# Mamba layer on one core: B products in two row groups of TensorE, C products in four column groups, units of half the channels

## The chip, the cores and the metric

The kernel runs on one core of a Trainium2 chip. The metric is the device time of one execution in microseconds (us). Before the change it is 13144.94 us, the median of three runs (13144.44 to 13147.74). A core has five engines that run side by side, each with its own queue of instructions in order: TensorE (PE; the loads of its stationary operand are shown as PEld), VectorE (DVE), ScalarE (ACT), GpSimd (POOL) and SyncE (SP), which here only issues DMA transfers. TensorE writes into PSUM, eight banks of 512 floats in each of 128 partitions; everything else lies in SBUF or in HBM.

## The reference

The input x has the shape (16, 64, 64, 128). Layer 0 adds to x a two-dimensional recurrent network over the group-normed x; layer 1 adds the sum of a forward and a backward Mamba scan over the group-normed result, with 4096 tokens an image. The change lies in layer 1 alone. Cut to what matters:

```python
def _mamba(x, in_w, conv_w, conv_b, x_w, dt_w, dt_b, A_log, D, out_w):
    xz = x @ in_w.T
    xc, z = jnp.split(xz, 2, axis=-1)
    ...
    xc = jax.nn.silu(jnp.transpose(xt, (0, 2, 1)))
    dbl = xc @ x_w.T
    dt, Bm, Cm = jnp.split(dbl, [DT_RANK, DT_RANK + D_STATE], axis=-1)
    dt = jax.nn.softplus(dt @ dt_w.T + dt_b)
    dA = jnp.exp(dt[..., None] * A)
    dBx = dt[..., None] * Bm[:, :, None, :] * xc[..., None]
    def step(h, inp):
        dA_t, dBx_t, C_t = inp
        h = dA_t * h + dBx_t
        y = jnp.einsum('bds,bs->bd', h, C_t)
        return (h, y)
    ...
    y = jnp.swapaxes(ys, 0, 1) + xc * D
    y = y * jax.nn.silu(z)
    return y @ out_w.T
```

For each of 16 states and 256 channels there is thus: a decay (exp), a drive (dt times x times B), a recurrence along the tokens, a product with C, and a sum over the states.

## The kernel before, in words

Layer 0 runs first. Layer 1 works in 256 passes: 16 images, 2 directions, 8 chunks of 512 tokens. In a pass the 256 channels are two halves of 128 partitions, and tokens lie along the free axis, but for the sums, which stand with tokens on partitions.

What one pass does, with the names of its methods: `conv` (line 1049) and `silu` (1060) make xc; `xproj` (1087) makes dt's input, B and C as rows, in two column groups of 64, each for one half of the tokens; `rows` (1103) writes B and C to HBM; `dtproj` (1137) and `softplus` (1148) make dt; `times` (1154, GpSimd) makes dtx = dt * xc; `turn` and `turn_take` (1161, 1170) make its transpose dtxt.

For each state s and half h, `decay` (1180, ACT) writes exp(dt * A) into SBUF (`das`) or a PSUM bank (`da`). The drive is made in one of three ways, by a letter for each state in `KINDS`: "P", GpSimd multiplies dtx with a row of B that a DMA spread over all partitions (`drive`, 1185); "M" and "T", ACT scales dtxt by B, token by token (`drive_turned`, 1192, with B's transpose from `bturn`, 1112), and TensorE transposes it back (`drive_back`, 1218); "N" and "U", B's row is scattered to a diagonal in HBM and loaded as `dg`, and TensorE multiplies dtxt with it (`drive_back`, 1209). `scan` (1230, VectorE) runs the recurrence over 512 tokens; its start value comes from `carry`, which `keep` (1245 or 1249) writes after the same scan of the pass before. `out_of` multiplies with a spread row of C, on GpSimd for both halves at once (1256) or, for "T" and "U", on VectorE (1258). `sums` (1265) adds the 16 products of a pass in PSUM (`py`) by transposes with the identity: 8 for each state. `skip`, `again`, `finish`, `back`, `project` and the rest complete the output.

The order of the instructions is made by a planner in the kernel (`order_of_issue` and `simulate`): it knows a cost of each step (`COST`), a due time (`URGENCY`), the number of buffers (`RINGS`) and how many PSUM banks each use may hold (`LIMIT`), and lists the steps in the order in which its own model would start them. Six PSUM banks serve all short uses, and two hold `py`. Queues keep that order on the chip and wait for one another by semaphores.

Of the kernel before, what the change touches and what calls it, by code (L numbers as in the profile page):

```python
# [14 lines left out]
P = 128  # L15
# [5 lines left out]
NH = DI // P  # L21
# [15 lines left out]
KINDS = ("MPNTMNPMUNPTMNPM", "MPMTPNMPTMPUMNPM")  # L37

RINGS = {
    "bank": 6, "py": 1, "das": 4, "dbx": 4, "dbt": 3, "dg": 3, "hst": 4, "hc": 5,  # L40
    "br": 4, "cr": 5, "xc": 2, "dt": 2, "dtx": 2, "dtxt": 2, "dbl": 2, "bt": 2, "z": 1, "y": 1,
    "yt": 1, "xr": 1, "xl": 1, "yo": 1, "yl": 1,
# [3 lines left out]
    "conv": 0.865, "gate": 0.87, "silu": 0.62, "softplus": 0.65, "gate_take": 0.6, "dtproj": 0.95,  # L46
    "xproj": 1.0, "xproj_take": 0.4, "bturn": 0.25, "bturn_take": 0.15, "times": 2.34,
    "turn": 0.47, "turn_take": 0.47, "decay": 0.62, "drive": 2.34, "drive_turned": 1.6,
    "drive_back": 0.44, "drive_back_diag": 0.88, "scan": 1.18,
    "keep_turned": 0.13, "keep": 0.6, "out_turned": 0.6, "out": 2.34, "sums": 0.88, "skip": 0.44,  # L50
# [7 lines left out]
LIMIT = {"misc": 2, "bank": 5}  # L58
# [6 lines left out]
        {(0, 0): -27.9, (0, 1): -55.24, (0, 2): -37.14, (0, 3): -26.5, (1, 0): -25.66, (1, 1): -31.09,  # L65
         (1, 2): -28.23, (1, 3): -24.41},
        {(0, 0): -34.48, (0, 1): -62.91, (0, 2): -27.86, (0, 3): -25.86, (1, 0): -33.52, (1, 1): -26.55,
         (1, 2): -34.72, (1, 3): -27.13},
    ),
    "xproj": (  # L70
        {(): -7.14},
        {(): 5},
    ),
    "xproj_take": (
        {(): -0.87},
        {(): -6.61},
    ),
    "rows": (
        {(): 6.65},
        {(): 22.72},  # L80
    ),
    "bturn": (
        {(): -69.81},
        {(): -79.06},
    ),
    "bturn_take": (
        {(): -11.43},
        {(): -18.91},
    ),
    "dtproj": (  # L90
        {(0,): -63.21, (1,): -27.76},
        {(0,): -42.3, (1,): -15.88},
    ),
    "times": (
        {(): -134.9},
        {(): -152.1},
    ),
    "turn": (
        {(0,): -117.7, (1,): -95.41},
        {(0,): -92.29, (1,): -73.14},  # L100
    ),
    "turn_take": (
        {(0,): -12.62, (1,): -21.64},
        {(0,): -15.32, (1,): -17.24},
    ),
    "decay": (
        {(0, 0): 1.62, (0, 1): -12.81, (1, 0): -13.82, (1, 1): -8.37, (2, 0): 9.59, (2, 1): 7.54,
         (3, 0): -3.93, (3, 1): -3.12, (4, 0): -25.4, (4, 1): 2.96, (5, 0): 16.41, (5, 1): 14.98,
         (6, 0): -14.89, (6, 1): -7.22, (7, 0): 17.61, (7, 1): 6.71, (8, 0): -49.21, (8, 1): -31.38,
         (9, 0): 30.2, (9, 1): 28.66, (10, 0): -15.29, (10, 1): -11.14, (11, 0): -39.1, (11, 1): -52.04,  # L110
         (12, 0): 11.3, (12, 1): 12.04, (13, 0): -4.72, (13, 1): -9.28, (14, 0): -8.46, (14, 1): 9.15,
         (15, 0): 6.51, (15, 1): 10.38},
        {(0, 0): -11.72, (0, 1): -13.95, (1, 0): -23.83, (1, 1): -23.36, (2, 0): 5.39, (2, 1): 3.65,
         (3, 0): -27.89, (3, 1): -33.87, (4, 0): -17.63, (4, 1): -10.29, (5, 0): -5.06, (5, 1): 8.98,
         (6, 0): -5.94, (6, 1): 4.1, (7, 0): 5.44, (7, 1): 12.02, (8, 0): -73.78, (8, 1): -77.71,
         (9, 0): 21.8, (9, 1): 10.89, (10, 0): -3.99, (10, 1): -15.28, (11, 0): -27.37, (11, 1): -37.65,
         (12, 0): 21.39, (12, 1): 9.09, (13, 0): -2.78, (13, 1): -3.97, (14, 0): -1.99, (14, 1): 19.81,
         (15, 0): 11.27, (15, 1): 19.92},
    ),
    "spread": (  # L120
        {("c", 0): -1.78, ("c", 1): -117.27, ("b", 1): -23.09, ("c", 2): -80.12, ("d", 2): -40.37,
         ("c", 3): -18.07, ("c", 4): -0.55, ("c", 5): -99.41, ("d", 5): -52.16, ("c", 6): -133.17,
         ("b", 6): -13.49, ("c", 7): -18.83, ("c", 8): -39.5, ("d", 8): 9.08, ("c", 9): -42.09,
         ("d", 9): -26.61, ("c", 10): -81.5, ("b", 10): -14.43, ("c", 11): -35.04, ("c", 12): -76.62,
         ("c", 13): -69.54, ("d", 13): 21.06, ("c", 14): -21.91, ("b", 14): -26.12, ("c", 15): -95.57},
        {("c", 0): -14.51, ("c", 1): -135.28, ("b", 1): -22.37, ("c", 2): -75.2, ("c", 3): 26.76,
         ("c", 4): -11.36, ("b", 4): -10.82, ("c", 5): -37.95, ("d", 5): 9.47, ("c", 6): -122.31,
         ("c", 7): -91.31, ("b", 7): -6.34, ("c", 8): -1.04, ("c", 9): -15.62, ("c", 10): -118.12,
         ("b", 10): -20.57, ("c", 11): -6.63, ("d", 11): 42.13, ("c", 12): -104.85, ("c", 13): -62.16,
         ("d", 13): 36.52, ("c", 14): -56.98, ("b", 14): -28.81, ("c", 15): -80.03},  # L130
    ),
    "drive_turned": (
        {(0,): 4.39, (3,): 8.43, (4,): -6.7, (7,): -0.75, (11,): 7.02, (12,): -6.99, (15,): -17.26},
        {(0,): -1.81, (2,): -23.9, (3,): -35.33, (6,): -11.17, (8,): -20.91, (9,): -60.49, (12,): 7.71,
         (15,): 0.83},
    ),
    "drive_back": (
        {(0, 0): 3.71, (0, 1): 1.89, (2, 0): -5.19, (2, 1): -6.19, (3, 0): -4.81, (3, 1): 0.01,
         (4, 0): -2.71, (4, 1): 0.38, (5, 0): -18.47, (5, 1): 5.45, (7, 0): 9.18, (7, 1): 10, (8, 0): 9.85,
         (8, 1): 10.09, (9, 0): 10.62, (9, 1): 10.75, (11, 0): 3.53, (11, 1): 12.69, (12, 0): 4.21,  # L140
         (12, 1): 14.29, (13, 0): 12.99, (13, 1): 14.53, (15, 0): 16.89, (15, 1): 17.89},
        {(0, 0): -2.14, (0, 1): -4.49, (2, 0): -12.32, (2, 1): 4.91, (3, 0): -12.93, (3, 1): -0.55,
         (5, 0): -12.51, (5, 1): -4.37, (6, 0): -3.25, (6, 1): -2.4, (8, 0): 4.69, (8, 1): -1.16,
         (9, 0): 7.45, (9, 1): 9.75, (11, 0): 10.55, (11, 1): 10.75, (12, 0): 11.8, (12, 1): 14.97,
         (13, 0): 16.19, (13, 1): 16.9, (15, 0): 18.18, (15, 1): 10.8},
    ),
    "scan": (
        {(0, 0): 70.25, (0, 1): 59.47, (1, 0): 8.22, (1, 1): 9.32, (2, 0): -9.21, (2, 1): -2.84,
         (3, 0): 51.28, (3, 1): 75.32, (4, 0): 55.73, (4, 1): 59.47, (5, 0): 137.02, (5, 1): 138.28,
         (6, 0): 27.09, (6, 1): 15.69, (7, 0): 32.24, (7, 1): 37.07, (8, 0): 94.24, (8, 1): 108.17,  # L150
         (9, 0): 0.44, (9, 1): 28.19, (10, 0): 73.98, (10, 1): 59.24, (11, 0): 106.87, (11, 1): 94.54,
         (12, 0): -14.38, (12, 1): 5.54, (13, 0): 148.93, (13, 1): 161.13, (14, 0): 96.47, (14, 1): 100.3,
         (15, 0): 3.43, (15, 1): -30.56},
        {(0, 0): 96, (0, 1): 81.85, (1, 0): 21.08, (1, 1): 15.17, (2, 0): -6.35, (2, 1): 2.5,
         (3, 0): 36.94, (3, 1): 50.72, (4, 0): 106.56, (4, 1): 99.08, (5, 0): 93.31, (5, 1): 110.65,
         (6, 0): -9.88, (6, 1): -0.78, (7, 0): 31.56, (7, 1): 34.1, (8, 0): 112.12, (8, 1): 144.28,
         (9, 0): -41.6, (9, 1): -10.42, (10, 0): 40.85, (10, 1): 31.68, (11, 0): 26.81, (11, 1): 19.41,
         (12, 0): 6.38, (12, 1): 39.24, (13, 0): 149.38, (13, 1): 149.05, (14, 0): 81.27, (14, 1): 88.98,
         (15, 0): 50.57, (15, 1): 7.33},
    ),  # L160
    "keep": (
        {(0,): -45.32, (1,): -38.3, (2,): -27.42, (3,): 18.46, (4,): -29.29, (5,): -21.12, (6,): -34.06,
         (7,): -33.8, (8,): -42.14, (9,): -10.39, (10,): -80.29, (11,): 59.69, (12,): -29.07,
         (13,): -54.07, (14,): -50.65, (15,): 7.31},
        {(0,): -50.47, (1,): -36.77, (2,): -54.91, (3,): 44.96, (4,): -38.14, (5,): -61.49, (6,): -11.86,
         (7,): -26.15, (8,): 8.91, (9,): 9.26, (10,): -17.81, (11,): -47.77, (12,): -17.89, (13,): -57.38,
         (14,): -65.8, (15,): 6.8},
    ),
    "out_of": (
        {(0,): 42.48, (1,): -101.16, (2,): -79.47, (3, 0): -31.43, (3, 1): -28.02, (4,): 51.12,  # L170
         (5,): 18.82, (6,): -90.94, (7,): -54.6, (8, 0): 19.29, (8, 1): 24.04, (9,): -47.79, (10,): -28.65,
         (11, 0): -12.07, (11, 1): -5.85, (12,): -67.16, (13,): -35.58, (14,): 28.33, (15,): -59.17},
        {(0,): 31.38, (1,): -101.73, (2,): -8.51, (3, 0): -36.58, (3, 1): -37.73, (4,): 25.8, (5,): -6.07,
         (6,): -58.81, (7,): -73.64, (8, 0): -9.83, (8, 1): 5.81, (9,): -32.35, (10,): -90.84,
         (11, 0): 16.76, (11, 1): 25.57, (12,): -65.96, (13,): -59.82, (14,): -25.53, (15,): -3.11},
    ),
    "sums": (
# [1224 lines left out]
```

## Time and profile before

| what | value |
|---|---|
| median of three runs | 13144.94 us |
| span of the profiled execution | 13233.8 us |
| PE busy, share of the span | 12901.2 us, 97% |
| DVE busy | 12067.0 us, 91% |
| ACT busy | 11513.4 us, 87% |
| POOL busy | 11261.4 us, 85% |
| DMA moved | 2025.28 MB |
| mean granted TensorE clock | 0.993 |

Shares of the whole span mix the two layers: layer 0 lasts to about 1590 us and leaves ACT and POOL half idle. Matmuls are pipelined, so the mean duration of one is longer than the distance to the next, and a busy PE is not PE at its peak. A group's line names the line of the kernel, the engine, the operation, out<-in with buffer numbers left out, the shapes, the count, then busy us and mean ns, then the idle time of the engine just before these instructions and what ended it.

### The profile page before, as it was taken

The numbers are of one execution on the slowest core, as the hardware profiler recorded it, in microseconds if no ns is written. First come the engines' busy times: TensorE is split into PE (matmuls) and PEld (weight loads), VectorE is DVE, ScalarE is ACT, GpSimd is POOL, SyncE is SP. The second block draws the span as 40 slices with busy tenths as digits, with TensorE's granted clock in tenths as the row PEclk, the third lists the DMA queues.
The fourth block names the chain that finished last, engine by engine and source line by source line (L and its number), as shares of the span: only waits on it lengthen the run. The fifth ranks groups of instructions, "written<-read, shape, count | busy, mean of one in ns | idle before, by whom it ended". The sixth has DMA issues, their size and how long they took to land. (4 is left out here: it accounts for less than half of the span.)

```text
span 13233.8 us, 263820 instructions
## 1 busy us (share of the span) xinstructions
PE 12901.2 (97%) x91444; PEld 10833.0 (82%) x91444; DVE 12067.0 (91%) x14353; ACT 11513.4 (87%) x21184; POOL 11261.4 (85%) x4996
## 2 busy tenths in 40 slices
PE   8999999999999999999999999999999999999999
PEld 7666788888888888888888888888888888888887
DVE  6776699999999999999999999999999999999998
ACT  3444599999999999999999999999999999999998
POOL 0111299999999999999999999999999999999998
PEclk8999999999999999999999999999999999999999
DMA  4222265656666666656566666666665656666665
GB/s 143 54 57 54 63 172 158 172 156 172 161 167 165 164 165 160 172 158 172 158 170 161 166 165 163 166 159 172 158 173 160 169 162 168 164 163 166 163 166 145
DMA packets 2777751, 2025.28 MB, mean 153 GB/s; under 512 B 1584848, under 2 KB 1930464, under 8 KB 2776416
## 3 DMA queue, kind: packets, MB, share of 16 engines
q1 hardware_dynamic: 2698464, 1973.16, 57.5%
q10 hardware_dynamic: 77952, 35.24, 1.1%
q8 instruction: 725, 11.88, 0.4%
q14 instruction: 610, 5.00, 0.1%
HBM read 1849.24 MB, written 157.02 MB: 152 GB/s over the span
## 5 line engine op out<-in xcount | busy, mean ns | idle before, releaser
L1256 POOL TENSOR_TENSOR hc<-hst,cr 128x1024 f32<-128x1024 f32 x3328 | 7800.2, 2374 | 327.7 <-DVE hst L1230 243.2
L1230 DVE TENSOR_TENSOR_SCAN hst<-das,carry,hps 128x512 f32<-128x512 f32 x3808 | 4668.3, 1261 | 190.3 <-PE hps L1218 93.8
L1265 PE MATMUL py<-ident,hc 128*128 128x128 f32 x32768 | 4150.1, 274 | 57.2 <-POOL hc L1256 56.5
L1265 PEld LDWEIGHTS py<-ident,hc 128*128 128x128 f32 x32768 | 3676.6, 141 | 451.7 <-issue 272.5
L1180 ACT ACTIVATE das<-dt,A_log_sb 128x512 f32<-128x512 f32 x5888 | 3875.9, 713 | 121.5 <-DVE hst L1230 79.2
L1192 ACT ACTIVATE dbt<-dtxt,bt 128x256 f32<-128x256 f32 x7680 | 3231.7, 498 | 159.0 <-PE hps L1218 146.9
L1185 POOL TENSOR_TENSOR dbx<-dtx,br 128x1024 f32<-128x1024 f32 x1152 | 2724.6, 2378 | 10.1
L1230 DVE TENSOR_TENSOR_SCAN hst<-da,carry,dbx 128x512 f32<-128x512 f32 x2016 | 2468.8, 1260 | 31.7 <-ACT da L1180 30.0
L1218 PE MATMUL hps<-ident,dbt 128*128 128x128 f32 x15360 | 2264.2, 274 | 133.8 <-DVE hc L1258 109.3
L1209 PE MATMUL hps<-dg,dtxt 128*128 128x128 f32 x16384 | 2175.2, 277 | 38.7 <-DVE hst L1230 20.2
L1218 PEld LDWEIGHTS hps<-ident,dbt 128*128 128x128 f32 x15360 | 1783.9, 141 | 463.6 <-issue 329.7
L1209 PEld LDWEIGHTS hps<-dg,dtxt 128*128 128x128 f32 x16384 | 2004.6, 192 | 119.1 <-DVE hst L1230 45.9
L1049 PE MATMUL pp<-xT,wk 128*128 128x512 f32 x4096 | 1900.9, 596 | 0.5 <-DVE xl L837 0.5
L1230 DVE TENSOR_TENSOR_SCAN hps<-das,carry,hps 128x512 f32<-128x512 f32 x1344 | 1654.3, 1265 | 20.3 <-PE hps L1209 10.6
L1180 ACT ACTIVATE da<-dt,A_log_sb 128x512 f32<-128x512 f32 x2304 | 1556.2, 683 | 79.7 <-DVE hst L1230 58.6
L816 POOL TENSOR_TENSOR a_f<-a_f,c 128x288 f32<-128x288 f32 (+40 forms) x254 | 211.6, 833 | 1341.2 <-ACT a_f L808 1274.0
L1258 DVE TENSOR_TENSOR hc<-hps,cr 128x512 f32<-128x512 f32 x1536 | 1025.2, 674 | 258.5 <-DMA cr<-rows 247.7
L1049 PEld LDWEIGHTS pp<-xT,wk 128*128 128x128 f32 x4096 | 716.5, 190 | 627.7 <-issue 605.3
L1154 POOL TENSOR_TENSOR dtx<-dt,xc 128x1024 f32<-128x1024 f32 x256 | 607.9, 2374 | 280.4 <-ACT dt L1148 275.5
L1230 DVE TENSOR_TENSOR_SCAN hst<-das,hps 128x512 f32<-128x512 f32 x544 | 641.6, 1203 | 82.8 <-issue 27.1
L808 ACT ACTIVATE a_f<-pg_f,b_sb 128x288 f32<-128x288 f32 (+40 forms) x508 | 217.3, 471 | 361.9 <-DMA x<-xl 161.5
L1137 PE MATMUL pv<-dbl,dt_wT 128*128 128x256 f32 x2048 | 507.2, 380 | 8.5 <-ACT xc L1060 8.5
(115 smaller groups left out, 12672.9 us busy)
## 6 DMA issues: line engine op xcount, KB each, us to landing
cr<-rows SPq DMA_DIRECT2D x4096, 256.0 KB
br<-rows SPq DMA_DIRECT2D x1152, 256.0 KB
dg<-diag SPq DMA_DIRECT2D x1024, 256.0 KB
yf<-yo SPq DMA_DIRECT2D x128, 512.0 KB
yl<-yf SPq DMA_DIRECT2D x128, 512.0 KB
carry<-hst SPq DMA_DIRECT2D x3328, 1.0 KB
xs<-in_x_dram SPq DMA_DIRECT2D x64, 512.0 KB
xr<-x SPq DMA_DIRECT2D x128, 256.0 KB
```

The lines of the kernel that those rows point to most:

```text
L1049: nc.tensor.matmul(self.ps["conv", h], lhsT=wk[:, k, h * P : (h + 1) * P], rhs=xT[self.b % 2][:, t0 : t0 + T], start=(k == 0), stop=(k == ...
L1137: nc.tensor.matmul(pv[:, q * TQ : (q + 1) * TQ], lhsT=dt_wT[:, q, h * P : (h + 1) * P], rhs=self.dbl, start=True, stop=True,)
L1154: nc.gpsimd.tensor_mul(self.dtx, self.dt, self.xc)
L1180: nc.scalar.activation(t, self.dt[:, h, :], AF.Exp, scale=amat[:, h, s : s + 1])
L1185: nc.gpsimd.tensor_mul(t, self.dtx, bc(self.brow.pop(s), 1, NH))
L1192: nc.scalar.activation(t[:, j, :], self.dtxt[:, j, :], AF.Copy, scale=self.bt[:, j, s : s + 1])
L1209: nc.tensor.matmul(t[:, j * P : (j + 1) * P], lhsT=self.dtxt[:, j, h * P : (h + 1) * P], rhs=self.dbt[s][:, j, :], start=True, stop=True,)
L1218: nc.tensor.transpose(t[:, j * P : (j + 1) * P], self.dbt[s][:, j, h * P : (h + 1) * P], ident)
L1230: nc.vector.tensor_tensor_scan(t[:, self.rev], self.da.pop((s, h))[:, self.rev], dbx[:, self.rev], 0.0 if self.first else carry[:, self.d, ...
L1256: nc.gpsimd.tensor_mul(self.hc[s], self.hst[s], bc(self.crow[s], 1, NH))
L1258: nc.vector.tensor_mul(self.hc[s][:, h, :], self.h[s, h], self.crow[s])
L1265: nc.tensor.matmul(self.py[:, j, cols], start=j not in self.banks, stop=last, skip_group_check=True, **how,)
```

## The change

The three ways by letters go. Of the 16 states the first eight (`NX`) form two groups of four ("X"), the other eight four pairs ("R"), and every unit works on one half of the channels. `ORDER` lists the units' scans.

- X: GpSimd makes the drives of two states at a time into a tile `group` of 512 tokens by 4 states, state innermost, so each write steps over 16 bytes. The decay goes to a PSUM bank; the scan runs in place in `group`. TensorE transposes `group` in blocks of 32 tokens by 4 states (`turned`), ACT copies the block out of PSUM (`turned_take`), and `weigh` multiplies it with a matrix that holds C's four rows on shifted diagonals (`cd`), which is the product with C and the sum over the four states in one. Each of its matmuls has 32 stationary columns and writes 32 partitions; four stand side by side in four column groups.
- R: one matrix `dg` holds two states' B for 64 partitions above and 64 below; `drive_rows` multiplies dtxt with it in two row groups of 64 partitions, each writing its own PSUM bank of a two-bank tile `pair`. dtxt is made with a step of four tokens, `dg`'s columns are read with a step of four floats, and the two states lie alternating in `pair`. The decays go to SBUF. `out_of` multiplies two states with two spread rows of C on GpSimd, `sums` is as before.
- `dtproj` uses two row groups and the `pair` tile; `silu` and `softplus` are two sessions on ACT, between which decays may stand. `keep` is a DMA for each unit. `bturn`, `drive_turned`, VectorE's `out_of` and `keep` go.
- Rings: four banks in place of six, one `pair` of two banks; `y` and `yo`, `xl` and `xr` share buffers. Due times are new throughout.

```diff
-KINDS = ("MPNTMNPMUNPTMNPM", "MPMTPNMPTMPUMNPM")
+GX = 4
+TB = P // GX
+NX = 8
+NG, NR = NX // GX, (NS - NX) // 2
+ORDER = ("00a00b11c11d22e22f33g33h", "00a00b11c11d22e22f33g33h")
 RINGS = {
-    "bank": 6, "py": 1, "das": 4, "dbx": 4, "dbt": 3, "dg": 3, "hst": 4, "hc": 5,
-    "br": 4, "cr": 5, "xc": 2, "dt": 2, "dtx": 2, "dtxt": 2, "dbl": 2, "bt": 2, "z": 1, "y": 1,
-    "yt": 1, "xr": 1, "xl": 1, "yo": 1, "yl": 1,
+    "bank": 4, "pair": 1, "py": 1, "das": 3, "dg": 3, "group": 3, "cd": 2, "ht": 6, "hst": 3, "hc": 4,
+    "br": 3, "cr": 2, "xc": 2, "dt": 2, "dtx": 2, "dtxt": 2, "dbl": 2, "z": 1, "y": 1,
+    "yt": 1, "xl": 1, "yl": 1,
 }
...
-LIMIT = {"misc": 2, "bank": 5}
+LIMIT = {"misc": 2, "bank": 2}
...
+            def dtproj(self):
+                pv = self.ps["dt"] = psum.tile([P, NQ, T], F32, name=f"pv_{self.nm}", tag="pair")
+                for h in range(NH):
+                    for q in range(NQ):
+                        rows = slice(q * QP, (q + 1) * QP)
+                        nc.tensor.matmul(
+                            pv[:, q, h * TQ : (h + 1) * TQ],
+                            lhsT=dt_wT[rows, h * P : (h + 1) * P],
+                            rhs=self.dbl[rows, :],
...
+                strided = self.dtx.rearrange("p h (i j) -> p h j i", j=NB)
                 for j in range(2):
                     for h in range(NH):
                         nc.tensor.transpose(
-                            pt[:, j, h * P : (h + 1) * P],
-                            self.dtx[:, h, (2 * i + j) * P : (2 * i + j + 1) * P],
-                            ident,
+                            pt[:, j, h * P : (h + 1) * P], strided[:, h, 2 * i + j, :], ident
                         )
...
+            def drive(self, q, h):
+                g, m = divmod(2 * q, GX)
+                if m == 0:
+                    self.group[g, h] = ring(sp, "group", [P, T, GX], f"group_{self.nm}_{g}_{h}")
+                both = self.group[g, h].rearrange("p t m -> p m t")
+                nc.gpsimd.tensor_mul(both[:, m : m + 2, :], bc(self.dtx[:, h, :], 1, 2), self.brow[q])
+                for k in range(2):
+                    self.dbx[2 * q + k, h] = both[:, m + k, :]
...
+            def drive_rows(self, g, h):
+                step = P // NQ
+                dg = self.mat["d", g].rearrange("p (i n j) -> p j i n", n=2, j=NB)
+                pair = psum.tile([P, NQ, T], F32, name=f"hps_{self.nm}_{g}_{h}", tag="pair")
                 for j in range(NB):
+                    for r in range(NQ):
+                        rows = slice(r * step, (r + 1) * step)
+                        half = pair[:, r, :].rearrange("p (i j n) -> p j i n", j=NB, n=2)
                         nc.tensor.matmul(
+                            half[:, j, :, :],
+                            lhsT=self.dtxt[rows, j, h * P : (h + 1) * P],
+                            rhs=dg[rows, j, :, :],
                             start=True,
                             stop=True,
+                            skip_group_check=True,
                         )
+                for k in range(2):
+                    self.dbx[NX + 2 * g + k, h] = pair.rearrange("p r t -> p (r t)")[:, k::2]
...
+            def out_of(self, g, h):
+                self.hc[g, h] = ring(sp, "hc", [P, 2, T], f"hc_{self.nm}_{g}_{h}")
+                nc.gpsimd.tensor_mul(self.hc[g, h], self.hst[g, h], self.crow[g])
+
+            def turned(self, g, h, j, place):
+                pt = self.ps["turned", g, h, j] = bank(place, f"ptg_{self.nm}_{g}_{h}_{j}", (P, GX, P))
+                for k in range(GX):
+                    t0 = (GX * j + k) * TB
+                    nc.tensor.transpose(
+                        pt[:, k, :],
+                        self.group[g, h][:, t0 : t0 + TB, :].rearrange("p t s -> p (t s)"),
+                        ident,
+                    )
+
+            def turned_take(self, g, h, j):
+                t = self.ht[g, h, j] = ring(sp, "ht", [P, GX, P], f"ht_{self.nm}_{g}_{h}_{j}")
+                nc.scalar.copy(t, self.ps.pop(("turned", g, h, j)))
+
+            def weigh(self, g, h):
+                cd = self.mat["k", g].rearrange("p (k t) -> p k t", t=TB)
+                for j in range(NB):
+                    for q in range(GX):
+                        c0 = (j % 2) * DI + h * P
                         nc.tensor.matmul(
+                            self.py[q * TB : (q + 1) * TB, j // 2, c0 : c0 + P],
+                            lhsT=cd[:, GX * j + q, :],
+                            rhs=self.ht[g, h, j][:, q, :],
+                            start=False,
+                            stop=False,
+                            skip_group_check=True,
                         )
```

## The prediction

> **What bounds the kernel now.** I read the busy time by stretches first, then the scan's first and last start, the groups, the order of time on TensorE around the tiled matmuls, and at last VectorE's groups by shape, for operands that step over 16 bytes.
>
> Layer 1 runs from the first scan to the last. Line 1230 by itself (duration shortest/median/longest in ns, first and last start):
>
> ```profile
> L1230 DVE TENSOR_TENSOR_SCAN hst<-das,carry,hps x3808: 1242/1256/1282, 1636.1 to 13217.6; 128x512 f32<-128x512 f32 x191
> ...
> L1230 DVE TENSOR_TENSOR_SCAN hst<-das,hps x544: 1187/1196/1222, 1595.4 to 12888.0; 128x512 f32<-128x512 f32 x182
> ```
>
> So (13217.6 - 1595.4) / 256 = 45.40 us for one pass; the 1595 us before belong to layer 0, which the change leaves alone. A stretch in the middle of layer 1 (busy time of PE, weight loads, DVE, ACT, POOL, clock, DMA):
>
> ```profile
> 6000.00:8000.00 2000.00, 1958.45 (x14555) 1677.64 (x14554) 1896.51 (x2016) 1871.78 (x3381) 1903.20 (x817) 1.00 0.64 165
> ```
>
> Per pass that is PE 44.5, DVE 43.1, ACT 42.5, POOL 43.2 of 45.4 us. Nobody has room: the engine that loses least, TensorE, idles 0.9 us a pass, and its clock is full. What the pass costs follows from the engine with the largest sum, plus an idle rest of about 1 us for coupling. The groups that the change touches:
>
> ```profile
> L1256 POOL TENSOR_TENSOR hc<-hst,cr 128x1024 f32<-128x1024 f32 x3328 | 7800.2, 2374 | 327.7 <-DVE hst L1230 243.2
> ...
> L1265 PE MATMUL py<-ident,hc 128*128 128x128 f32 x32768 | 4150.1, 274 | 57.2 <-POOL hc L1256 56.5
> ...
> L1192 ACT ACTIVATE dbt<-dtxt,bt 128x256 f32<-128x256 f32 x7680 | 3231.7, 498 | 159.0 <-PE hps L1218 146.9
> L1185 POOL TENSOR_TENSOR dbx<-dtx,br 128x1024 f32<-128x1024 f32 x1152 | 2724.6, 2378 | 10.1
> ...
> L1218 PE MATMUL hps<-ident,dbt 128*128 128x128 f32 x15360 | 2264.2, 274 | 133.8 <-DVE hc L1258 109.3
> L1209 PE MATMUL hps<-dg,dtxt 128*128 128x128 f32 x16384 | 2175.2, 277 | 38.7 <-DVE hst L1230 20.2
> ...
> L1258 DVE TENSOR_TENSOR hc<-hps,cr 128x512 f32<-128x512 f32 x1536 | 1025.2, 674 | 258.5 <-DMA cr<-rows 247.7
> ```
>
> Divide the counts by 256: a pass has 128 transposes for the sums, 60 transposes and 64 half matmuls for the drives (an fp32 matmul is two instructions; 32 matmuls show as 64), 30 copies on ACT. The mean duration of a matmul is its latency; what counts is start to start. In order of time on TensorE:
>
> ```profile
> 6001.19 1.04 PE L1265 MATMUL py<-ident,hc 128*128 128x128 f32 x8
> 6002.06 1.06 PE L1209 MATMUL hps<-dg,dtxt 128*128 128x128 f32 x8
> 6002.95 1.04 PE L1265 MATMUL py<-ident,hc 128*128 128x128 f32 x8
> ```
>
> Eight transposes take 6002.06 - 6001.19 = 0.87 (0.109 each), eight half matmuls of 128 columns 0.89 (0.112 each). And the one place that already splits the array, xproj, in two column groups:
>
> ```profile
> 6039.74 0.27 PE L1218 MATMUL hps<-ident,dbt 128*128 128x128 f32 x1
> 6039.94 1.08 PE L1087 MATMUL pd<-xc,x_wT_sb 128*64 128x256 f32 x8
> 6040.96 1.97 PE L1265 MATMUL py<-ident,hc 128*128 128x128 f32 x16
> ```
>
> Eight half matmuls of 256 columns, twice 0.108 = 0.216 each, would be 1.73 one after another and 0.86 in pairs. They take 1.02 to the next start, and begin 0.20 after a transpose that normally takes 0.109. So pairs do run side by side, and entering and leaving the split costs 1.02 - 0.86 + 0.09 = about 0.24 a burst.
>
> **The change on TensorE.** Removed: 60 transposes of turned drives (6.54), 64 half matmuls with diagonals (7.17), 64 of 128 transposes of the sums (6.98), bturn's two (0.22), eight unsplit halves of dtproj (1.73): 22.64 us. Added: 64 transposes of groups (6.98); dtproj in two row groups, 0.86 + 0.24 = 1.10; weigh, four bursts of 32 halves in four column groups, 8 steps of 0.112 + 0.24 = 1.14 each, 4.54; drive_rows, eight bursts of 16 halves in two row groups. If a step of a pair takes 0.112, such a burst is 8 x 0.112 + 0.24 = 1.14, and eight are 9.09. Then 21.71 are added and TensorE is 0.93 shorter.
>
> But drive_rows streams dg, whose columns now stand 4 floats apart (layout i, n, j; one j at a time), so every element lies in another 16 bytes; and turn loads dtx with the same step. No matmul of this trace reads so. The nearest row is VectorE's line 928, one of whose operands steps over 4 floats, against line 834 without:
>
> ```profile
> L834 DVE TENSOR_TENSOR xl<-ph,xl 128x384 f32<-128x384 f32 x64 | 35.4, 553 | 13.8 <-PE ph L831 11.1 <-DMA xl<-in_x_dram 2.1 <-issue 0.2
> L834 DVE TENSOR_TENSOR xl<-ph,xl 128x256 f32<-128x256 f32 x64 | 27.1, 424 | 57.5 <-PE ph L831 39.1 <-DMA xl<-in_x_dram 17.3 <-PE pt L779 0.5
> L834 DVE TENSOR_TENSOR xl<-ph,xl 128x128 f32<-128x128 f32 x64 | 18.4, 288 | 37.6 <-PE ph L831 36.3 <-DMA xl<-in_x_dram 1.3
> ...
> L928 DVE TENSOR_TENSOR wk<-in_wT,xT 128x256 f32<-128x256 f32 x4 | 2.4, 604 | 0.0
> ```
>
> Line 834 has (553 - 288) / 256 = 1.035 ns an element and 156 ns fixed; line 928 then (604 - 156) / 256 = 1.75 ns, 1.69 times as much. TensorE asks for an element every 0.112 / 128 = 0.87 ns, faster than VectorE, so it should feel a limit on steps at least as much. Bounds for one step: 0.112 (no penalty) and 128 x 1.75 ns = 0.224 (the same time per element). I take the ratio, 0.112 x 1.69 = 0.189, between the two. A burst is then 8 x 0.189 + 0.24 = 1.75, eight 14.0 (9.09 to 16.3), and turn's eight 8 x 0.109 x 1.69 = 1.47 in place of 0.87 (to 1.79). Sum: 21.71 + 4.91 + 0.60 - 22.64 = +4.6 us a pass; at the upper end +7.2 + 0.9 - 0.9 = +7.2. That two row groups overlap as column groups do is shown nowhere: one after the other a burst is 16 x 0.112 + 0.24 = 2.03, the same upper end. If four column groups only ran as two, weigh would gain 4 x 0.9 = 3.6.
>
> The Trainium skill's "SBUF — State Buffer", section "Door 1: The DMA port swizzle", speaks both ways here. It has 16-byte lines that want at least two hits, as line 928 shows with 604 against 424 ns, but then calls a stride of 4 fp32 free, which is the step used here and which line 928 contradicts. By its "free", the sum would be -0.93 a pass.
>
> **The other engines.** VectorE loses six products (1025.2 / 1536 = 0.667 each, 4.0) and six copies of a carry (line 1245, 166.0 / 1536 = 0.108, 0.65): 38.4 left. Sixteen of its 32 scans now read and write in place with a 16-byte step. A scan takes (1196 - 156) / 512 = 2.03 ns an element already, more than 1.75, so I take no extra; the bound is 512 x 0.72 = 0.37 each, 5.9 in all, 44.3. GpSimd goes from 18.5 to 17 instructions of 2.375: 39.6. Eight of them write with the step; it spends 2.3 ns an element, so again nothing, and at most 8 x 1024 x 0.72 ns = 5.9, 45.5. A gain is excluded for both, as the element counts stay. ACT loses 30 copies of 0.421 (12.6) and bt (0.2), gains 16 copies out of PSUM at line 1170's 271.2 / 512 = 0.53 (8.5), and, since silu and softplus are now two sessions with decays between, one more table load of 1.28 (four a pass in the new order): 39.5. DMA moves 5.5 in place of 6.1 MB a pass, with some 2300 more small packets, at a share of 0.64: no bound. All of this is hidden under a TensorE of 49.
>
> On the Trainium skill's "GPSIMD Engine Reference", "Performance pitfalls for Q7 kernels": it prices reads that step over more than 8 bytes at about half more, and says nothing on writes, which no row here shows. Put on eight writes, an estimate, it would add 8 x 1.19 = 9.5 and make GpSimd 49.
>
> The moved waits: drive_rows waits for the single pair tile, which two scans (2.45) and once a pass dtproj's softplus hold; behind it on TensorE's queue stand the group transposes and sums that ACT and later passes wait for. 8 x (1.75 + 2.45 + about 0.3) + 4 = 40 us stays below 49.
>
> **Sum.** 45.4 + 4.6, less 0.5 of the 0.9 idle that a longer TensorE no longer meets, is 49.5: +4.1 x 256 = +1050 us. The profiled span is 13233.8, 0.7% above the median 13144.9 of the runs; the difference is put on the median: **14200**.
>
> **Rivals.** (1) Steps cost TensorE nothing and row groups overlap: TensorE 0.93 shorter, others at 38 to 40, so some idle goes too; -0.9 to -1.5 a pass, 12,760 to 12,910. For it: xproj's pairs overlap; against: line 928. It decides as long as a step stays below about 0.125 (0.93 / 72 more). (2) TensorE is free but GpSimd's stepped write (or the scans) takes the upper price: 45.5 plus the 2.2 that it idles now is 47.7, +590, 13,730. Against it: both are slower per element than line 928's rate. (3) Row groups run one after the other, or a step costs its whole time: +7.2 less 0.5, +1715, 14,860. For: no row shows row groups. (4) The order fits badly, with one pair tile and four banks in place of six: half to one us of idle eats the 0.93, 13,050 to 13,250.
>
> **Chances.** The forecast (13,900 to 14,500) 0.38, rival 1 0.29, rival 2 0.11, rival 3 0.14, rival 4 0.08. A measurement tells 0.2% (26 us) from no change. Faster 0.31 (rival 1 and some of 4), same 0.03, slower 0.66. The range reaches from rival 1's faster side to rival 3: 12,760 to 14,880; the forecast's own is 13,900 to 14,500.
>
> **What would show it.** hps at line 1260: starts of pairs 0.19 apart and bursts of 1.75 us; at 0.11 and 1.14 the forecast is wrong and rival 1 or 4 holds; single starts 0.11 apart with no pairs mean rival 3. Scans on group above 1.3 us, or POOL group<-dtx,br above 2.5, mean rival 2. TensorE above 98% busy with DVE, ACT and POOL near 80% would confirm who bounds; pv and py bursts of 1.1 the tiling's price.

## The result: 14,947 us, and the profile after

| | before | after |
|---|---|---|
| median of the runs | 13144.69 us (4 runs) | 14947.03 us (4 runs, 14944.65 to 14953.69) |
| ratio | 1 | 1.1372, 95% interval 1.1356 to 1.1388 |
| profiled span | 13233.8 us | 14945.6 us |
| from one pass to the next | 45.40 us | 52.13 us |
| PE / DVE / ACT / POOL in a pass | 44.5 / 43.1 / 42.5 / 43.2 us | 51.4 / 39.5 / 39.9 / 40.2 us |

The change makes the kernel 13.7% slower. The pass is read from the scans again: the list of line 1280's instructions in the kernel after, with shortest/median/longest duration in ns and first and last start.

```profile
L1280 DVE TENSOR_TENSOR_SCAN hst<-das,carry,hps x3584: 1252/1258/1283, 1639.1 to 14930.5; 128x512 f32<-128x512 f32 x200
L1280 DVE TENSOR_TENSOR_SCAN group<-da,group x512: 1196/1200/1230, 1585.5 to 14563.0; 128x512 f32<-128x512 f32 x171
```

(14930.5 - 1585.5) / 256 = 52.13 us, 6.73 more than before. 6.73 x 256 = 1723 us, where the medians lie 1802 us apart. The profiled execution of before was itself 89 us longer than the median of before, and that of after was not, which covers the other 80 us. Next the stretch that the prediction read before, in the kernel after (busy time of PE, weight loads, DVE, ACT, POOL, then clock, DMA share, GB/s):

```profile
6000.00:8000.00 2000.00, 1970.64 (x17668) 1504.91 (x17668) 1517.03 (x1289) 1531.69 (x2406) 1544.08 (x654) 1.00 0.49 132
```

TensorE is at 98.5%, at full clock, and everything else has fallen to 76 or 77%. The table's busy times are these times 52.13 / 2000. So the four engines, level before, are level no more: TensorE alone sets the pass. Which of its work does, the groups of the page say:

```profile
L1303 POOL TENSOR_TENSOR hc<-hst,cr 128x1024 f32<-128x1024 f32 x2048 | 4889.3, 2389 | 1905.0 <-DVE hst L1280 1004.3
L1280 DVE TENSOR_TENSOR_SCAN hst<-das,carry,hps 128x512 f32<-128x512 f32 x3584 | 4394.0, 1267 | 2187.9 <-PE hps L1260 1478.9
L1223 POOL TENSOR_TENSOR group<-dtx,br 128x1024 f32<-128x1024 f32 x2048 | 4886.1, 2398 | 423.6 <-PE ptg L1310 235.6
L1280 DVE TENSOR_TENSOR_SCAN group<-da,carry,group 128x512 f32<-128x512 f32 x3584 | 4392.0, 1263 | 352.3 <-ACT da L1215 313.2
L1260 PE MATMUL hps<-d,dtxt 64*128 64x128 f32 x32768 | 4229.1, 411 | 44.6 <-DVE hst L1280 31.1
```

Read the idle times first. VectorE sat 2188 us idle before the scans of the R states, 1479 of them until `hps`, the product of drive_rows at line 1260, came; GpSimd waited in turn for those scans. Then the durations: a scan that reads and writes `group` with a step of 16 bytes takes 1263 ns, one that does not 1267; GpSimd's stepped write takes 2398 ns against 2389. In the kernel before, a scan with the same sources but without the step (`hst<-da,carry,dbx`) took 1260 ns, and GpSimd's packed write of a drive 2378. So the scan does not pay for the step, and GpSimd pays 20 ns of 2398 at most. TensorE's matmul does pay: 411 ns of latency where a packed one of 128 columns took 277. In order of time on TensorE, in the kernel after:

```profile
6009.71 2.07 PE L1260 MATMUL hps<-d,dtxt 64*128 64x128 f32 x16
6011.71 0.66 PE L1310 MATMUL ptg<-ident,group 128*128 128x128 f32 x4
6012.29 1.08 PE L1326 MATMUL py<-ht,k 128*32 128x128 f32 x32
6013.31 1.23 PE L1197 MATMUL ptx<-ident,dtx 128*128 128x128 f32 x8
6014.47 2.07 PE L1260 MATMUL hps<-d,dtxt 64*128 64x128 f32 x16
6016.47 1.08 PE L1129 MATMUL pd<-xc,x_wT_sb 128*64 128x256 f32 x8
```

A burst of drive_rows, 16 half matmuls in eight pairs, takes 6011.71 - 6009.71 = 2.00 us. In the records of its single matmuls the two of a pair start 0.003 to 0.010 us apart, so the two row groups do run side by side. The second pair follows the first after 0.29 us, and every later pair follows after 0.227 (called 0.226 from here on): twice the 0.112 of a packed matmul. The 32 halves of `weigh` in four column groups take 1.02, the eight of `turn` 1.16.

### The profile page after: what moved, and what is told of

Read it like the earlier page. It is cut to its first block, busy times and chain, and to the rows that moved or that the text cites. A ratio compares the mean times of both kernels' runs of the same rounds, so it can differ in the third digit from the quotient of the medians.

```text
span 14945.6 us, 315691 instructions
## 1 busy us (share of the span) xinstructions
PE 14655.8 (98%) x124724; PEld 11116.4 (74%) x124724; DVE 11199.4 (75%) x11281; ACT 10874.0 (73%) x17599; POOL 10507.2 (70%) x4612
## 5 line engine op out<-in xcount | busy, mean ns | idle before, releaser
L1303 POOL TENSOR_TENSOR hc<-hst,cr 128x1024 f32<-128x1024 f32 x2048 | 4889.3, 2389 | 1905.0 <-DVE hst L1280 1004.3
L1280 DVE TENSOR_TENSOR_SCAN hst<-das,carry,hps 128x512 f32<-128x512 f32 x3584 | 4394.0, 1267 | 2187.9 <-PE hps L1260 1478.9
L1223 POOL TENSOR_TENSOR group<-dtx,br 128x1024 f32<-128x1024 f32 x2048 | 4886.1, 2398 | 423.6 <-PE ptg L1310 235.6
L1280 DVE TENSOR_TENSOR_SCAN group<-da,carry,group 128x512 f32<-128x512 f32 x3584 | 4392.0, 1263 | 352.3 <-ACT da L1215 313.2
L1260 PE MATMUL hps<-d,dtxt 64*128 64x128 f32 x32768 | 4229.1, 411 | 44.6 <-DVE hst L1280 31.1
L1260 PEld LDWEIGHTS hps<-d,dtxt 64*128 64x128 f32 x32768 | 3202.5, 199 | 806.7 <-issue 467.2
L1318 ACT COPY ht<-ptg 128x512 f32<-128x512 f32 x4096 | 2277.4, 588 | 1347.2 <-PE ptg L1310 1177.9
L1310 PE MATMUL ptg<-ident,group 128*128 128x128 f32 x16384 | 2356.8, 280 | 129.2 <-ACT ht L1318 125.2
L1310 PEld LDWEIGHTS ptg<-ident,group 128*128 128x128 f32 x16384 | 1789.6, 141 | 706.1 <-issue 309.9
L1338 PE MATMUL py<-ident,hc 128*128 128x128 f32 x16384 | 2073.1, 275 | 6.4 <-POOL hc L1303 6.4
L1338 PEld LDWEIGHTS py<-ident,hc 128*128 128x128 f32 x16384 | 1819.3, 141 | 345.1 <-issue 281.8
```

The costliest lines, as they stand in the source:

```text
L1223: nc.gpsimd.tensor_mul(both[:, m : m + 2, :], bc(self.dtx[:, h, :], 1, 2), self.brow[q])
L1260: nc.tensor.matmul(half[:, j, :, :], lhsT=self.dtxt[rows, j, h * P : (h + 1) * P], rhs=dg[rows, j, :, :], start=True, stop=True, skip_grou ...
L1280: nc.vector.tensor_tensor_scan(t[:, self.rev], self.da.pop((s, h))[:, self.rev], dbx[:, self.rev], 0.0 if self.first else carry[:, self.d, ...
L1303: nc.gpsimd.tensor_mul(self.hc[g, h], self.hst[g, h], self.crow[g])
L1310: nc.tensor.transpose(pt[:, k, :], self.group[g, h][:, t0 : t0 + TB, :].rearrange("p t s -> p (t s)"), ident,)
L1318: nc.scalar.copy(t, self.ps.pop(("turned", g, h, j)))
```

## The experiments

Each kernel below ran beside the kernel before on its own chip; there before took 13,229 (e1 to e4), 13,233 (e5 to e8), 13,231 (e9, e10) and 13,195 us (e11, e12). In e1 to e3, e5 to e7, e10 and e11 the drives of the R states are other numbers; e4, e8, e9 and e12 compute all that the kernel after does.

### Reading or writing, or the weights?

Three suspects for the 0.226: the step of the moving operand (S), the writes that leave gaps in PSUM (W), and the loads of stationary operands of two row groups side by side (L).

e1, the moving operand read packed:

```diff
-                            rhs=dg[rows, j, :, :],
+                            rhs=self.mat["d", g][rows, j * P : (j + 1) * P],
```

> The changed kernel, but drive_rows streams 128 neighbouring columns of dg in place of columns 4 floats apart; PSUM is written as before. The drives of the eight R states are then other numbers (the matrix keeps its old layout); the instructions are the same in number and size. Theory S (the 16-byte step of the moving operand sets the pair step of 0.226 us): pair steps of 0.11, bursts at line 1260 of about 1.15 in place of 2.0, hps 9 us a pass in place of 15.9, and a total of 13,100 to 13,300. Theory W (the PSUM writes in pairs of floats with gaps set it): 0.226 stays, 14,900 to 15,000. Theory L (weight loads of two row groups of 128 columns set it): 0.226 stays, 14,900 to 15,000.

13,600.99 us in one run, where e2 below, slow as the kernel after, took 14,965 on the same chip: 1,364 of the 1,736 us over before are gone, from one operand's order in SBUF. The timeline of TensorE in e1:

```profile
6001.25 1.16 PE L1260 MATMUL hps<-d,dtxt 64*128 64x128 f32 x16
6002.34 5.42 PE L1091 MATMUL pp<-xT,wk 128*128 128x512 f32 x12
```

The burst takes 1.09 us in place of 2.00, and past the first, pairs start 0.112 apart. S holds for the price of a pair. The time is another matter: it lies 300 us above the 13,100 to 13,300 that S gave, and the sections below look for the rest.

e2, the output written packed, and e3, both:

```diff
-                            half[:, j, :, :],
+                            pair[:, r, j * P : (j + 1) * P],
```

> The changed kernel, but each matmul of drive_rows writes 128 neighbouring floats of its PSUM bank in place of pairs 8 floats apart; the moving operand keeps its step. The drives of the R states stand in another order of tokens. Theory S: pair steps stay at 0.226 us and the total at 14,900 to 15,000. Theory W: pair steps of 0.11 and 13,100 to 13,300. Theory L: nothing changes.

> Both edits of the two runs beside it; the R drives are again other numbers. Theory S: like the packed read alone within 30 us. Theory W: like the packed write alone. If both steps limit on their own, only this run falls, to 13,100 to 13,300. Theory L: 0.226 and 14,900 to 15,000 here too.

e2 took 14,964.71 us with pairs 0.226 apart and 52.18 us from pass to pass, as the kernel after; e3 took 13,606.71, as e1, and so again more than S gave. The gaps in these PSUM writes, which put two floats side by side and leave out the next six, cost nothing here. Since e1 loads the same weights in the same groups, L falls too.

e8, whether each stream pays alone or only two side by side: the loops exchanged, so that the lower row group follows the upper.

```diff
-                for j in range(NB):
-                    for r in range(NQ):
+                for r in range(NQ):
+                    for j in range(NB):
```

> The kernel after with the loops of drive_rows exchanged: all matmuls of the upper 64 rows first, then all of the lower, so that the two row groups run one after the other; same step of four floats, same result. If each stream pays for its own step, 16 matmuls of 0.226 us make a burst of 3.6-3.8 us, 29-30 us a pass in place of 15.9, and the time is 18,300-18,800. If the price comes from two groups reading with a step side by side, 16 matmuls of 0.112 make 1.8 us, and the time stays within 14,800-15,100.

17,377.77 us. In e8's timeline a burst takes 2.98 us, not 3.6:

```profile
6005.57 3.04 PE L1260 MATMUL hps<-d,dtxt 64*128 64x128 f32 x16
6008.55 1.09 PE L1310 MATMUL ptg<-ident,group 128*128 128x128 f32 x8
```

The single records show why. The first four matmuls run alone and start 0.227 to 0.297 us apart, and the last four, alone again, 0.227 apart, so each stream pays its own step and no second group is needed for it. In the middle, eight matmuls start in two interleaved rows, each with 0.227 us from one to the next (0.07 and 0.15 us between neighbours in turn). The records do not name the group, but by the program's order these are the second group's first four under the first group's last four. That is where the other 0.6 us of the expected burst went, and the expected 18,300 to 18,800 us missed this overlap.

e7, how far the step may go: every second float in place of every fourth.

```diff
-                dg = self.mat["d", g].rearrange("p (i n j) -> p j i n", n=2, j=NB)
+                dg = self.mat["d", g][:, : T // 2].rearrange("p (i n j) -> p j i n", n=2, j=2)
...
-                            rhs=dg[rows, j, :, :],
+                            rhs=dg[rows, j % 2, :, :],
```

> The kernel after with the moving operand of drive_rows read with a step of two floats (8 bytes) from the first half of dg (the drives of the R states are other numbers). If any step costs its full price, a pair of matmuls stays 0.226 us apart and the time is 14,930-14,980. If the price follows the bytes that a read of 16 covers, a pair is 0.112 to 0.12 us apart and the time 13,590-13,700; something between would be 0.15-0.19 us.

13,606.43 us, pairs 0.114 apart, and in e7's timeline a burst of 1.11 us:

```profile
6000.90 1.18 PE L1260 MATMUL hps<-d,dtxt 64*128 64x128 f32 x16
6002.01 1.09 PE L1310 MATMUL ptg<-ident,group 128*128 128x128 f32 x8
```

A step of 8 bytes is all but free here, a step of 16 doubles the time of a pair.

### Can the order in memory be had for nothing?

e4 computes everything and lays the matrix out in the order in which it is read, so the scatter of B writes single floats, and in 16 issues a pass in place of 8:

```diff
-                        dst = bass.AP(
-                            t.tensor, t.offset + k * NB, [[T + 2 * NB, step], [step * T, NQ], [1, NB]]
-                        )
...
+                        for r in range(NQ):
+                            dst = bass.AP(t.tensor, t.offset + r * step * T + k, [[T + 2, step], [P, NB]])
...
-                            rhs=dg[rows, j, :, :],
+                            rhs=self.mat["d", g][rows, j * P : (j + 1) * P],
```

> The whole computation, with the matrix laid out j, i, n, so that drive_rows reads packed columns; the scatter then writes single floats in place of runs of four, and is two transfers for each state in place of one (8 more issues on SP's queue and 3072 more small packets a pass; DMA share 0.49 in the changed kernel). Theory S: as the packed read alone plus at most 50 us, 13,100 to 13,350, about the kernel before. Theories W and L: 14,900 to 15,050. If the small packets bound it: pair steps of 0.11 but DMA waits at line 1260 and above 13,400.

A miss: 14,770.84 us, 1.1165 of before (1.1146 to 1.1184). The matmuls are cured, with bursts of 1.09 us as in e1 though every drive is right, and something else has come in, as e4's waits show (us in all, times, longest):

```profile
POOL hc L1302 <- DMA cr<-rows: 1648.6, 192, 13.5
...
PEld py L1337 <- POOL hc L1302: 811.5, 218, 10.6
PE py L1337 <- POOL hc L1302: 722.2, 190, 10.3
```

GpSimd waits for rows of C that a DMA brings late, and TensorE's sums wait for GpSimd. The granted TensorE clock is lower as well: from 6000 to 8000 us it is 0.95 in e4, against 0.99 in e1 and 1.00 in the kernels before and after. How much of e4's time is the slower clock and how much the waits themselves, no run here separates. e1 has the same wait for C's rows, smaller:

```profile
POOL hc L1303 <- DMA cr<-rows: 684.0, 177, 9.0
...
PEld py L1338 <- POOL hc L1303: 313.1, 143, 6.9
PE py L1338 <- POOL hc L1303: 276.1, 118, 6.7
```

### What makes the rows of C late

e5: packed reading, and the scatters of B left out after the first three passes.

```diff
                 if kind == "d":
+                    if self.number >= SETS:
+                        return
```

> Packed reading as in e1, and the B rows are scattered in the first three passes only (later passes drive the R states with old rows of B); eight DMAs of small packets fewer in a pass. If what e1 keeps above the kernel before (13,601 against 13,229) is lateness of C's rows behind these scatters, the 684 us that GpSimd waits for cr fall below 150 and the time to 13,200-13,400. If it is TensorE's own work (95% busy) and its mode switches, the time stays within 13,530-13,610.

13,225.33 us, 0.9995 of before (0.9983 to 1.0006): all that e1 kept above before is gone, and so is most of the wait.

```profile
POOL hc L1305 <- DMA cr<-rows: 130.1, 79, 3.6
```

e6 keeps the scatters and gives C's rows a third buffer (`"cr": 3`):

> Packed reading as in e1, three buffers for C's rows in place of two, all transfers kept. Lateness of C's rows: the wait of hc for cr falls from 684 us below 200 and the time to 13,300-13,450. TensorE's own work: 13,560-13,620 with the wait gone elsewhere.

13,432.34 us, 1.0152 of before (1.0122 to 1.0181). It is within the first theory's range, at its edge: the wait of hc for cr is no longer among the larger ones, but GpSimd now waits for `br`, B's spread rows, which come by the same queue, longer than e1's 200 us.

```profile
POOL group L1223 <- DMA br<-rows: 423.0, 122, 6.5
```

e10 keeps issues, waits and bytes, and replaces each scatter by a plain copy of 2 KB; e11 makes one copy of 4 KB for two states. Both after the first three passes:

```diff
+                        if self.number >= SETS:
+                            dst = bass.AP(t.tensor, t.offset + k * T, [[1, T]])
+                            src = bass.AP(self.dram.tensor, self.dram.offset + (st + k) * T, [[1, T]])
```

In e11 the copy is `[[1, 2 * T]]` on both sides for k = 0, and none for k = 1.

> Packed reading as in e1; after the first three passes each scatter of a B row is a plain copy of the same 2 KB into one row of the matrix (the drives of the R states are other numbers): same issues, same waits, same bytes, but no runs of 16 bytes. If the packets make C's rows late, the time falls to e5's 13,225 (13,210-13,300). If the issues and their waits on SP's queue do, it stays at e1's 13,570-13,620.

> As e10, but the two rows of B of a pair of states are copied by one issue of 4 KB (four issues a pass for the B rows, against eight in e10 and none in e5; after the first three passes, so the drives of the R states are other numbers). If SP's issues cost the time, it lies between e5 and e10, near the middle: 13,330-13,420. If what costs is only that something is written into the matrix before its load (the wait for it), four issues are as dear as eight: 13,490-13,540.

| B rows, issues a pass | ratio to before (interval) |
|---|---|
| none (e5) | 0.9995 (0.9983 to 1.0006) |
| 4 plain copies (e11, 13,288.91 us) | 1.0073 (1.0050 to 1.0096) |
| 8 plain copies (e10, 13,522.60 us) | 1.0222 (1.0198 to 1.0247) |
| 8 scatters of 16 bytes (e1, 13,600.99 us, one run) | 1.028 |

e10 landed between its two expectations. By the table the eight issues, with what waits for them, are worth about 2.3%, and the small packets about 0.6%, the latter from e1's single run. e11 fell below both of its ranges, also when its ratio is put on e10's before (13,328 us): its place between e5 and e10 is a third of the way, not the middle. But four issues are clearly cheaper than eight, which speaks against the wait for a written matrix as the whole price. The timeline of SP's queue in e1 shows how the issues can harm (start, duration; a number behind x says how many are drawn together):

```profile
6034.96 0.32 SPq L1160 DMA_DIRECT2D cr<-rows  x1
...
6045.09 1.23 SPq L1242 DMA_DIRECT2D d<-rows  x2
6046.37 2.02 SPq L1249 DMA_DIRECT2D k<-rows  x2
6048.44 3.36 SPq L1242 DMA_DIRECT2D d<-rows  x2
6051.85 0.59 SPq L1160 DMA_DIRECT2D br<-rows  x1
6052.48 1.18 SPq L1242 DMA_DIRECT2D d<-rows  x2
6053.76 0.64 SPq L1292 DMA_DIRECT2D carry<-hst  x1
6054.44 1.97 SPq L1242 DMA_DIRECT2D d<-rows  x2
...
6059.49 0.33 SPq L1160 DMA_DIRECT2D cr<-rows  x1
```

Here the queue is taken up for eleven microseconds, from 6045.09 to 6056.41, and 9.8 of them are issues of scatters: eight for B's rows (7.74) and two for C's (2.02). An issue usually takes about 0.6 us, and when several follow one another some take two or more. Between two loads of C there are 24.5 us in place of the usual ten or so. SP as a whole has time: it issues for some 25 of 47 us a pass, about as before the change (24.2 of 45.4). So it seems to be the bunch in one place, with two buffers for C where there were five half as large, that makes the load late. Fewer issues (e11, e5) and a third buffer (e6) each bring the time down; the same issues spread over the pass were not run.

The last two kernels compute everything. e9 puts tokens in pairs, so that TensorE reads with e7's free step and the scatter writes 8 bytes at a time, in 16 issues, with the third buffer; e12 gives half of these issues to ScalarE's queue.

```diff
-    "br": 3, "cr": 2,
+    "br": 3, "cr": 3,
...
+                        for a in range(2):
+                            dst = bass.AP(
+                                t.tensor, t.offset + 2 * k + a * T // 2, [[T + 4, step], [step * T, NQ], [1, 2]]
+                            )
...
+                            (nc.sync if a == 0 else nc.scalar).dma_start(dst, src)
...
-                dg = self.mat["d", g].rearrange("p (i n j) -> p j i n", n=2, j=NB)
+                dg = self.mat["d", g].rearrange("p (a i n b) -> p a b i n", a=2, n=2, b=2)
...
-                            rhs=dg[rows, j, :, :],
+                            rhs=dg[rows, j // 2, j % 2, :, :],
```

The line with `nc.scalar` is e12's; e9 issues both by `nc.sync`.

> The whole computation, with tokens in pairs in the matrix of B (order: pair of tokens, row, state, token of the pair), so that TensorE reads it with a step of two floats, which e7 showed at the packed price; the scatter writes runs of 8 bytes, twice the packets of the kernel after (262,144 more) and 16 issues a pass in place of 8; three buffers for C's rows as in e6. TensorE: a pair of matmuls 0.112 us apart. If the packets price the lateness (e4's 819,200 more cost 1,170 us over e1, so about 375 here, less what the third buffer covers), the time is 13,450-13,810. If the doubled issues alone do the harm, as in e4, it is 14,300 or more.

> The whole computation as in e9, but 8 of its 16 scatters a pass are issued by ScalarE's queue in place of SP's. If SP's queue, in which they stand before the loads of C's rows, makes e9 slow (14,058), SP's issue time falls from 31.5 to about 26 us a pass, the wait of hc and sums for C's rows shrinks towards e6's, and the time to 13,500-13,800, with ACT 5 us a pass fuller (8 issues of 0.64 us). If the small packets do the harm, they are the same and the time stays within 13,950-14,150; if ScalarE's own queue is held up by the issues and their waits, the time is above 14,100.

e9 took 14,057.93 us, 1.0624 of before (1.0603 to 1.0645): better than the kernel after, between its two expectations, and slower than before. Eight more issues of SP and twice the packets come with some 630 us over e6; GpSimd waits 788 us for `br`, and VectorE 683 for a carry, which goes through the same queue. The granted clock is lower again (0.97 in the mean of the execution, against 0.99 in e6). e12 took 15,094.91 us, 1.1439 (1.1413 to 1.1465): the third of its cases. In e12's waits ScalarE, held by scatters that stand in its queue, is late with decays and copies:

```profile
PEld ptg L1311 <- ACT ht L1319: 1135.9, 529, 8.7
...
ACT da L1215 <- DMA d<-rows: 861.6, 192, 8.3
```

SP's issue time did fall as expected, to 25.8 us a pass, but ScalarE's waits, and a granted clock of 0.93, hide whatever that gained. So e12 does not tell whether a free queue would have cured e9. No kernel here that computes everything has both prices away; a planner that spreads the scatters over the pass was not tried.

## Why the prediction was wrong

The direction and the mechanism were right: slower, by the step of drive_rows' moving operand, with TensorE above 98% and the rest near 77%. The time, 14,947, lies 747 above the forecast and 67 above the range. Two terms of the sum were too small: the price of a stepped pair, and the transposes of the groups. Point by point:

- **The step's price** is the term that failed. The prediction had 0.112 to 0.224 for a pair and took 0.189, VectorE's ratio of 1.69. It is 0.226: as the prediction's upper bound (0.224, from the 1.75 ns an element of VectorE's line 928), not as the ratio. The argument that TensorE should feel the limit "at least as much" spoke for the upper end, and the middle was taken. The two rows compared also differ in more than the step: line 834 reads one operand from PSUM, line 928 reads both from SBUF, so their ratio is not the step's alone. drive_rows takes 15.96 us a pass, start to start, in place of 14.0. With 0.226 the same sum gives about 14,800.
- **The transposes of the groups** are the second term that was too small. Start to start in 6000 to 12000 us, summed by group, a pass of TensorE is:

| us a pass | before | after | e1 | e5 |
|---|---|---|---|---|
| drives (hps) | 14.45 | 15.96 | 8.92 | 8.78 |
| sums: hc's transposes | 14.92 | 7.41 | 8.61 | 7.69 |
| sums: groups' transposes (ptg) | - | 8.64 | 8.77 | 8.73 |
| sums: weigh | - | 4.23 | 4.30 | 4.30 |
| all the rest | 16.02 | 15.95 | 16.40 | 16.05 |
| pass | 45.39 | 52.19 | 47.00 | 45.55 |

The groups' transposes were priced at 64 x 0.109 = 6.98 and take 8.64. For 125 us in all, 0.5 a pass, TensorE stands still before them until ACT has emptied a bank, as the waits of the kernel after show:

```profile
PE ptg L1310 <- ACT ht L1318: 125.2, 252, 2.6
```

About 0.6 us a pass more lies between such a transpose and the tiled burst behind it; the rest of the 1.66 was not followed up. The 0.24 for entering and leaving a burst was not too small: a burst of drive_rows takes 2.00 where 8 x 0.226 + 0.24 is 2.05, and one of weigh 1.02 in place of 1.14. So of the 2.7 us by which the table's pass (52.19) exceeds the 49.5 of the sum, drive_rows is 1.96 and the groups' transposes are 1.66; hc's transposes add 0.4, and all else together came out 1.3 lower.

- **Rival 1** (free steps, 12,760 to 12,910) fails even with its condition given. With packed reading and no late rows (e5) the drives are 5.7 us a pass shorter, the sums 5.8 longer, and the time is that of before. The groups' transposes, 1.75 above their price there, take more than the whole saving of 0.93.
- **Rival 2** fell: scans pay nothing and GpSimd next to nothing, as the prediction took it. The reason given, that both are slower per element than line 928's rate, was not tested by itself.
- **Rival 3** had two halves under one price. "The step costs its whole time" is what happened (14,860 given); "row groups run one after the other" is not.
- **Rival 4** (an order that fits badly) names in part what is left once the step is cured. Its 13,050 to 13,250 does not follow from its own half to one us of idle, which less the 0.93 gives 13,035 to 13,165. e5, whose 0.9995 of before is 13,138 on the prediction's base, lies inside both, and TensorE's waits for a bank before the groups' transposes are of the kind it named. e1's 13,601 is beyond it, and what e1 has over e5 came from SP's queue and C's buffers, which it did not name.
- **turn's stepped load** was put at 1.47 and is 1.15. Here the step is in the stationary operand. Its load does take longer, 209 ns (PEld, line 1197) where before it took 141 (line 1161), but most of that overlaps with matmuls: eight of them start 0.121 us apart in place of 0.109. weigh (4.23 for 4.54) and dtproj (1.07 for 1.10) were sized well, and so were the other engines: DVE 39.5 for 38.4, ACT 39.9 for 39.5, POOL 40.2 for 39.6.
- **DMA** was called no bound, by its share (0.64, now 0.49). Under TensorE's 52 us it is hardly one: GpSimd waits 213 us for C's rows, and TensorE 44 for hc. With the step cured, e1 lies 372 us above before and e5, without the scatters, does not. That is a matter of issues in one queue and of buffers, which the share does not show.
- **The base**: 1050 us were added to the median, though taken from a profiled span 89 us longer. That is some 80 of the 747 us, and enough by itself for the 67 above the range.

## What to carry to other kernels

Before laying data out for a cheap DMA, look at the side that streams it, here at 0.87 ns an element: a moving operand with one float in 16 bytes cost TensorE twice the time, and with two it cost next to nothing extra. VectorE's price, taken over as time per element, came close (0.224 for 0.226) and as a ratio did not; that is one case, and a plain doubling of 0.112 says the same. Price a regrouping of the sums whole, with what the new transposes wait for; with packed reading (e5) the drives gained what the sums lost. And when DMA looks idle, still count what one queue issues in one place, and how many buffers stand between it and the load that comes next.

## What the runs showed of the hardware that was not expected

- The same step of 16 bytes costs TensorE's moving operand 0.226 in place of 0.112 us for 128 columns (e1 against the kernel after), its stationary operand 0.01 us from start to start (0.121 against 0.109 in turn, though the load itself takes 209 ns in place of 141), a scan nothing (1263 against 1260 to 1267 ns) and GpSimd's write 9 to 20 ns of 2398. A step of 8 bytes costs the moving operand next to nothing (0.114 for 0.112, e7).
- The Trainium skill's "SBUF — State Buffer", "Door 1: The DMA port swizzle", wants two accesses in every 16-byte line for full rate. e7 and the kernel after agree with that: two floats a line run at 0.114, one at 0.226. Its remark that a stride of 4 fp32 is free disagrees with the same 0.226. It also says that PSUM access with gaps slows matmuls; e2, packed, has its pairs 0.226 us apart as the kernel after with its gaps. Those gaps lie between pairs of floats, 8 bytes each, and gaps between single floats were not run.
- The two matmuls of a pair in row groups of 64 start 0.003 to 0.010 us apart and keep their pace side by side. As e8's records read, a second group's matmuls also start while the first group's last ones still run, without being interleaved in the program.
- An SP issue of a 2 KB transfer takes 0.6 us, as a scatter (e1) or as a plain copy (e10) alike, and when several follow one another some take two or more. Eight of the plain ones a pass cost 2.3% of the time (e10 against e5), with the DMA engines busy 55% of it.
- The clock granted to TensorE differs from run to run: from 6000 to 8000 us it is 0.95 in e4 and 0.93 in e12, where TensorE is busy for 90 and 88% of the stretch, and 1.00 in the kernel after, at 98.5%. But e8, 98.9% busy, has 0.96, so idle time is not all that goes with a lower clock.
